# Two-layer graph attention on one core: the first batch's adjacency tiles converted on ScalarE beside the weight setup

## The chip, the cores and the metric

The kernel runs on one core of a Trainium2 chip. The metric is the device time of one execution in microseconds (us), as the median of several runs; lower is better. The engines are named as in the profile: PE (TensorE), DVE (VectorE), ACT (ScalarE), POOL (GpSimd) and SP, whose queue issues the DMAs here.

## The reference, cut to what matters

There are 16 batches of 1024 nodes with 64 features, and a 0/1 adjacency matrix `adj` (16 x 1024 x 1024, int32, about 8 neighbours in a row beside the diagonal). Layer 0 is graph attention with 8 heads, layer 1 graph attention with additive scores; each is followed by a residual and a layer norm.

```python
# layer 0: per head, over neighbours alone
q, k, v = x @ Wq + bq, x @ Wk + bk, x @ Wv + bv
scores = leaky_relu(q @ k.T / sqrt(64) + edge_bias[adj], 0.2)
attn = softmax(where(adj > 0, scores, -1e9))
x = layernorm(x + (attn @ v) @ Wp + bp)
# layer 1
hp = x @ lin_w.T + lin_b
e[i, j] = a . leaky_relu(W1 hp_i + W2 hp_j, 0.2)
x = layernorm(x + elu(softmax(where(adj > 0, e, -9e15)) @ hp))
```

The query and key weights only meet as products (`Wq Wk^T`, `Wq bk`, `Wk bq`, `bq . bk`), and so do `Wv` and `Wp`. The kernel forms these products once, ahead of the batches.

## The kernel before

**Setup.** The weights come in by DMA and are transposed on PE (`wqT`, `wkT`, `wvT`). Then a loop over the 8 heads (lines 107 to 124) forms the products in PSUM and DVE copies them out: `aqk` (64 x 64 per half, L118), `wvp` (L119), `qb` (L122), `wc1` (L124), and `wc8` (L121). `wc8[p, i, h, j]` is the column `Wq bk` of head `h`, where `i == j`, and zero elsewhere, for `i`, `j` below 8; it is cleared by a memset on POOL, and then each head writes 8 columns in each of two halves of the partitions, one instruction a column. The products go through a PSUM pool `ps_c` of 4 banks, two banks a head, so PE comes back to a bank when DVE has read it. Behind the loop come the scores' constants (`wc_row`, `wcb`), layer 1's weights (`lin2`, `w1h`, `w2d`, `rows_b` at L182), and the tables of the sparse form (`wz`, `rep_q`, `ident_b`, `no_diag`). The scratch of the setup is in the pool `tmp`. It and `ps_c` are closed at the end of the setup, and the pools of the groups (`per`, `dbl`, `sml`, the PSUM pools) are opened after that.

**Turning a batch's adjacency into lists** (`prepare`, L307 on). `adj` comes in 16 tiles of 128 rows x 512 columns, in two halves `hs` of 8 tiles. A tile `ad` (L300) has 4 buffers; load `k + 4` is issued after conversion `k`. Each is converted from int32 to bf16 (L325):

```python
nc.vector.tensor_scalar(ab[:, T, :, :], ad, 1.0 - TINY, 0.0, ALU.subtract, ALU.max)
```

which makes a one into `TINY` = 2^-20 and a zero into zero. In half of the tiles POOL clears the diagonal (L328). `ab` holds the 8 tiles of a half and has one buffer. PE sums the tiles of a half, weighted by `wz`, into `pat` (L334, 8 matmuls of 512 columns), DVE makes sort keys `ka` of it (L339), and then the lists of neighbours by max and match-replace instructions (L345 to L383). The lists go to DRAM (`col_d`, `slot_d`) and come back spread over the partitions (`cb` L468, `rows_s` L416). In the middle of its sorting, a batch issues the next batch's loads of `xs`, `dg` (the diagonal) and the first four `ad` tiles.

**The groups.** Eight groups of 128 rows per batch and layer. DVE turns `cb` into 0/1 columns `f` (L480), PE gathers the neighbours' features by matmuls with them (`pg`, L504), then come the scores, exponentials, weights and sums. The order of all engines in this part is written out by hand (a manual schedule): `prepare(0)` and `finish(0)` in full first, then the loop over the groups, with layer 1 of a batch 12 groups behind its layer 0, and `prepare` of the next batch cut into pieces between them. The setup ahead of that is ordered by the scheduler. Each engine does its instructions in the order in which they stand.

If a batch doesn't fit the sparse form, flags (`bad`) make the kernel run a second, dense path at the end; with these inputs it isn't run.

Of the kernel before, what the change touches and what calls it, by code (L numbers as in the profile page):

```python
# [9 lines left out]
F32 = mybir.dt.float32  # L10
I32 = mybir.dt.int32
AF = mybir.ActivationFunctionType
ALU = mybir.AluOpType
# [9 lines left out]
GR = 8  # L23
# [5 lines left out]
TINY = 2.0**-20  # L29
# [4 lines left out]
def kernel(  # L34
# [4 lines left out]
    nc = tc.nc  # L39
    B, N, D = x.shape  # L40
    H = edge_bias.shape[1]
    HD = H * D
    P = 128
# [7 lines left out]
    dram = ctx.enter_context(tc.tile_pool(name="dram", bufs=2, space=bass.MemoryType.DRAM))  # L51
    fast = ExitStack()
    fst = fast.enter_context(tc.tile_pool(name="fst", bufs=1))
    setup = ExitStack()
    ps_c = setup.enter_context(tc.tile_pool(name="ps_c", bufs=4, space=bass.MemoryType.PSUM))
    tmp = setup.enter_context(tc.tile_pool(name="tmp", bufs=1))
    ident = cst.tile([P, P], F32, name="ident")
    make_identity(nc, ident)
    eps = cst.tile([P, 1], F32, name="eps")
# [1 line left out]
    ones = cst.tile([P, P], F32, name="ones")  # L61
    nc.gpsimd.memset(ones, 1.0)


    def sub(n):
        return slice(n * D, n * D + D)
# [6 lines left out]
    def bank(name):  # L73
        return ps_c.tile([P, 4, P], F32, tag="c", name=f"ps_{name}")

    def halves(name, cols_):

        t = fst.tile([P] + cols_, F32, tag=name, name=name)
        nc.gpsimd.memset(t, 0.0)
        return t  # L80
# [21 lines left out]
    QS1 = 1.0 / float(D) ** 0.5  # L102
    aqk = halves("aqk", [2, H, D])
    wvp = fst.tile([P, H, D], F32, name="wvp")
    qb = fst.tile([P, H], F32, name="qb")
    wc8 = halves("wc8", [GR, H, GR])
    wc1 = tmp.tile([1, H], F32, name="wc1")
    for h in range(H):
        c, r = h // 2, sub(h % 2)
        pw = bank(f"h_{h}")  # L110
        pc = bank(f"hc_{h}")
        for n in range(2):
            o = sub(n)
            nc.tensor.matmul(pw[o, 0, 0:D], wqT[r, c, :], wkT[r, c, :], start=True, stop=True)
            nc.tensor.matmul(pw[o, 1, 0:D], wvT[r, c, :], wp_l[r, c, :], start=True, stop=True)
            nc.tensor.matmul(pw[o, 2, 0:1], wkT[r, c, :], bq_c[r, c : c + 1], start=True, stop=True)
            nc.tensor.matmul(pw[o, 3, 0:1], wqT[r, c, :], bk_c[r, c : c + 1], start=True, stop=True)
            nc.vector.tensor_scalar(aqk[o, n, h, :], pw[o, 0, 0:D], QS1, None, ALU.mult)  # L118
            nc.vector.tensor_copy(wvp[o, h, :], pw[o, 1, 0:D])  # L119
            for i in range(GR):  # L120
                nc.vector.tensor_scalar(wc8[o, i, h, i : i + 1], pw[o, 3, 0:1], QS1, None, ALU.mult)  # L121
        nc.vector.tensor_scalar(qb[:, h : h + 1], pw[:, 2, 0:1], QS1, None, ALU.mult)  # L122
        nc.tensor.matmul(pc[0:1, 0, 0:1], bq_c[r, c : c + 1], bk_c[r, c : c + 1], start=True, stop=True)
        nc.vector.tensor_scalar(wc1[:, h : h + 1], pc[0:1, 0, 0:1], QS1, None, ALU.mult)  # L124
    eb1 = tmp.tile([1, H], F32, name="eb1")
    nc.sync.dma_start(eb1, edge_bias[1:2, :])
    nc.vector.tensor_tensor(wc1, wc1, eb1, ALU.add)
# [4 lines left out]
    pw = bank("wcb")  # L132
# [7 lines left out]
    pw = bank("bpv")  # L140
# [15 lines left out]
    pw = bank("ww")  # L156
# [7 lines left out]
    pw = bank("lin")  # L164
    for n in range(2):
        o = sub(n)
# [7 lines left out]
    pw = bank("ub")  # L174
# [5 lines left out]
    pw = bank("rows_b")  # L180
# [53 lines left out]
    jrow = fst.tile([P, SEG // P], F32, name="jrow")  # L234
    nc.gpsimd.iota(jrow, [[-P, SEG // P]], base=SEG, channel_multiplier=-1, allow_small_or_imprecise_dtypes=True)

    bad = cst.tile([P, 1], F32, name="bad")
    nc.vector.memset(bad, 0.0)
    root = fst.tile([P, 1], F32, name="root")
# [16 lines left out]
    MULT = 4  # L256
    XX = mybir.AxisListType.X

    per = fast.enter_context(tc.tile_pool(name="g_per", bufs=1))
    dbl = fast.enter_context(tc.tile_pool(name="g_dbl", bufs=2))  # L260
    sml = fast.enter_context(tc.tile_pool(name="g_sml", bufs=4))
    ps_g = fast.enter_context(tc.tile_pool(name="ps_g", bufs=2, space=bass.MemoryType.PSUM))
    ps_s = fast.enter_context(tc.tile_pool(name="ps_s0", bufs=2, space=bass.MemoryType.PSUM))
    ps_p = fast.enter_context(tc.tile_pool(name="ps_p", bufs=2, space=bass.MemoryType.PSUM))
    ps_z = fast.enter_context(tc.tile_pool(name="ps_z", bufs=1, space=bass.MemoryType.PSUM))

    def by_rows(ap, n):
        return ap[n * 512 : n * 512 + 512, :].rearrange("(t r) d -> r t d", r=D)
# [40 lines left out]
    def prepare(b):  # L309
# [10 lines left out]
        for hs in range(2):  # L320
            ab = per.tile([P, NT, 2, SEG], BF16, tag="ab", name=f"ab_{b}_{hs}")
            for T in range(NT):
                ad = ads.pop(hs * NT + T)

                nc.vector.tensor_scalar(ab[:, T, :, :], ad, 1.0 - TINY, 0.0, ALU.subtract, ALU.max)  # L325
                if T % 4 // 2 == hs:
                    own = ab[:, T, T // 4, ts(T % 2, P)]
                    nc.gpsimd.tensor_tensor(own, own, no_diag, ALU.mult)  # L328
                load(hs * NT + T + 4)
                if T % 2:  # L330
                    yield "sums" if T == NT - 1 else None
            pat = ps_z.tile([P, 2, SEG], F32, tag="z", name=f"pat_{b}_{hs}")
            for T in range(NT):
                nc.tensor.matmul(  # L334
                    pat.rearrange("p a c -> p (a c)"), wz[:, P - NGT - NGT * T : 2 * P - NGT - NGT * T],
                    ab[:, T, :, :].rearrange("p n (t r) -> p t n r", r=D), start=(T == 0), stop=(T == NT - 1),
                )
            yield "keys"
            nc.vector.scalar_tensor_tensor(  # L339
                ka[:, 2 * hs : 2 * hs + 2, 0:SEG], pat, float(KEY), revc.unsqueeze(1).to_broadcast([P, 2, SEG]),  # L340
                ALU.mult, ALU.add,
            )
            yield
            for s in range(2 * hs, 2 * hs + 2):
                nc.vector.max(lst[:, s, 0:8], ka[:, s, 0:SEG])  # L345
                nc.vector.match_replace(kb[:, s, 0:SEG], lst[:, s, 0:8], ka[:, s, 0:SEG], -1.0)
                yield
# [114 lines left out]
    class Tiles:  # L462


        def load(self, t):
            nm = f"{self.b}_{self.layer}_{t}"
            self.cb[t] = cb = dbl.tile([P, NSEG, 2, NQ, WIN], BF16, tag="cb", bufs=3, name=f"cb_{nm}")
            nc.sync.dma_start(  # L468
                cb.rearrange("p s n q k -> p (s n q k)"),
                edges[self.b][t].rearrange("s n q k -> (s n q k)").unsqueeze(0).to_broadcast([P, NSEG * 2 * NQ * WIN]),  # L470
            )
# [382 lines left out]
    class Lists:  # L854


        def __init__(self):
            def parts():
                for b in range(1, B):
                    yield from prepare(b)  # L860
                    yield

            self.work = parts()
            self.done, self.part, self.side = 0, None, []
# [16 lines left out]
    with tc.manual_schedule(engines={getattr(mybir.EngineType, e) for e in order}):  # L881
        for _ in prepare(0):
            pass
# [10 lines left out]
        for g in range(NT * B + LAG + 7):  # L894
            u = g - LAG
            b, t = divmod(g, NT)
# [472 lines left out]
```

## Time and profile before

| | |
|---|---|
| time, median of 3 runs | 2506.59 us (2506.02 to 2509.31) |
| the profiled execution's own time | 2508.34 us |
| its span | 2506.5 us |
| busy, share of the span | PE 92%, PE weight load 78%, DVE 77%, ACT 58%, POOL 40% |
| the conversions L325 | 256 on DVE, 35.6 to 2106.2 us, median 422 ns |
| loads of `ad` (L300) | 256 of 256 KB, on SP's queue |
| first gather matmuls (L504) | at 94 us |

The span is the time from the profile's first instruction to its last; the profiled execution's time has in addition what lies around it. Rows of the timeline give start and duration in us, engine, line, operation, what is written and read, and in brackets how long the engine was idle before, and what ended that. A chain of waits follows from the last instruction back to what released each step. Rows of the page's groups have busy us in total and mean ns of one after the bar.

### The profile page before, as it was taken

To read this page: it belongs to the slowest core of one execution; us is meant where nothing else is said; L and a number is where in the kernel's file an instruction comes from. 1 tells how busy PE (TensorE), PEld (TensorE's weight loads), DVE (VectorE), ACT (ScalarE), POOL (GpSimd) and SP (SyncE) were. 2 spreads that over 40 slices of the span, in tenths; PEclk is the share of its full clock that TensorE was granted. 3 is DMA by queue.
4 is the path that set the end of the run, shared out by engine and by line. 5 is a ranking of instruction groups with operands and counts; after the bars stand their busy time and mean duration, and the time that the engine had idled before them with its cause. 6 is when DMAs were issued, how large, how long until landed. Compare 5 with 4: busy or idle time off the path is not lost.

```text
span 2506.5 us, 111153 instructions
## 1 busy us (share of the span) xinstructions
PE 2296.7 (92%) x48706; PEld 1951.9 (78%) x48706; DVE 1930.4 (77%) x5237; ACT 1450.3 (58%) x4401; POOL 1010.8 (40%) x1490
## 2 busy tenths in 40 slices
PE   5377999999999999999999999999999999999996
PEld 3266778888887888878888887878888887888864
DVE  6586868888887888888788878878787887866543
ACT  0054565666565665656566665656566665666743
POOL 1033433535344353534445353444534444443431
PEclk9988999999999999999999999999999999999998
DMA  3313242333224233323324232332423233231211
GB/s 102 109 43 117 81 143 77 104 116 109 91 81 138 77 117 103 121 77 100 120 77 140 81 119 77 113 107 78 142 86 113 83 111 103 66 96 61 69 38 29
DMA packets 192705, 239.03 MB, mean 95 GB/s; under 512 B 91732, under 2 KB 157332, under 8 KB 192212
## 3 DMA queue, kind: packets, MB, share of 16 engines
q1 hardware_dynamic: 192212, 231.85, 30.3%
q8 instruction: 384, 6.29, 1.0%
q14 instruction: 109, 0.89, 0.1%
HBM read 226.58 MB, written 5.21 MB: 92 GB/s over the span
## 4 chain that ended last, share of the span: by engine, by line
PE 66%; DVE 25%; DMA 3%; ACT 2%; issue 2%; POOL 1%; SPq 0%; POOLq 0%; ACTq 0%; DVEq 0%
PE pg L504 21%; PE s L616 5%; PE pt L523 5%; PE z L668 5%; DVE r L762 4%; PE pz L750 4%; PE pp L658 4%; PE pa L801 4%; PE pq L599 4%; PE pz L756 4%; PE po L684 3%; PE e L776 3%; DVE f L480 3%; DMA ad<-in_adj_dram 2%; PE pat L334 2%
## 5 line engine op out<-in xcount | busy, mean ns | idle before, releaser
L504 PE MATMUL pg<-f,x 128*64 128x272 bf16 (+2 forms) x13312 | 806.1, 273 | 40.4 <-DVE f L480 34.6
L504 PEld LDWEIGHTS <-x 128*64 128x64 bf16 x13312 | 662.8, 109 | 119.2 <-issue 73.8
L650 POOL TENSOR_TENSOR ls<-ls,den 128x480 f32<-128x480 f32 x256 | 298.5, 1166 | 579.8 <-DVE den L649 577.0
L510 ACT COPY xg<-pg 128x448 f32<-128x448 f32 x512 | 271.8, 531 | 392.4 <-PE pg L504 392.2
L480 DVE TENSOR_SCALAR f<-cb,jrow 128x2176 bf16<-128x2176 bf16 x512 | 409.0, 843 | 1.2 <-DMA cb<-col_d 1.0
L642 ACT ACTIVATE ls<-ls,mx 128x120 f32<-128x120 f32 x1024 | 391.2, 386 | 0.0
L524 ACT COPY xn<-pt 120x512 f32<-120x512 f32 x512 | 277.9, 598 | 22.7 <-PE pt L523 21.0
L523 PE MATMUL pt<-ident,xg 128*120 128x128 f32 x2048 | 269.6, 274 | 0.4
L761 ACT ACTIVATE r<-pz 128x480 f32<-128x480 f32 x256 | 132.2, 568 | 220.3 <-PE pz L756 220.3
L523 PEld LDWEIGHTS pt<-ident,xg 128*120 128x120 f32 x2048 | 229.4, 138 | 7.3 <-ACT xg L510 2.8
L489 POOL COPY xg<-xT 128x64 f32<-128x64 f32 x256 | 98.8, 396 | 307.1 <-PE pt L523 307.1
L762 DVE SCALAR_TENSOR_TENSOR r<-pz,r 128x480 f32<-128x480 f32 x256 | 155.9, 651 | 74.9 <-ACT r L761 74.6
L624 DVE TENSOR_TENSOR sc<-s,rowc 128x480 f32<-128x480 f32 x256 | 155.5, 649 | 71.2 <-PE s L616 69.3
L642 ACT ACTIVATION_READ_ACCUMULATOR ls<-ls,mx 128x1 f32 x1024 | 194.5, 190 | 0.0
L558 POOL TENSOR_TENSOR rs<-mv,eps 128x2 f32<-128x2 f32 x128 | 32.3, 253 | 379.0 <-DVE den L649 299.4
L632 DVE SCALAR_TENSOR_TENSOR ls<-sc 128x480 f32<-128x480 f32 x256 | 175.7, 686 | 0.0
L633 DVE TENSOR_REDUCE mx<-ls 128x4 f32<-128x480 f32 x256 | 167.2, 653 | 8.8
L756 PEld LDWEIGHTS pz<-rw,ub 64*64 64x64 f32 x4096 | 118.8, 133 | 63.2 <-issue 62.2
L600 DVE TENSOR_TENSOR qp<-pq,qb 128x512 f32<-128x512 f32 x128 | 88.2, 689 | 102.2 <-PE pq L599 101.0
L668 PE MATMUL z<-w,xn 120*64 120x64 f32 x4096 | 160.2, 229 | 4.8 <-ACT w L660 4.0
L658 PE MATMUL pp<-ident,ls 128*120 128x128 f32 x1024 | 143.0, 281 | 22.9 <-POOL ls L650 16.0
L668 PEld LDWEIGHTS z<-w,xn 120*64 120x64 f32 x4096 | 139.0, 141 | 28.6 <-ACT w L660 26.0
(212 smaller groups left out, 4092.7 us busy)
## 6 DMA issues: line engine op xcount, KB each, us to landing
cb<-col_d SPq DMA_DIRECT2D x271, 544.0 KB
ad<-in_adj_dram SPq DMA_DIRECT2D x256, 256.0 KB
xs<-in_x_dram SPq DMA_DIRECT2D x32, 128.0 KB
rows_s<-slot_d SPq DMA_DIRECT2D x256, 14.0 KB
out_dram<-o SPq DMA_DIRECT2D x32, 128.0 KB
col_d<-col SPq DMA_DIRECT2D x128, 4.2 KB
dg<-in_adj_dram SPq DMA_DIRECT2D x32, 2.0 KB
slot_d<-slot SPq DMA_DIRECT2D x16, 28.0 KB
```

Source lines behind the costliest of these rows:

```text
L480: nc.vector.tensor_scalar(fj.rearrange("p s n q k -> p (s n q k)"), cb.rearrange("p s n q k -> p (s n q k)"), jrow[:, j : j + 1], None, AL ...
L504: nc.tensor.matmul(pg[sub(n), :, FIRST * a_ + lo : FIRST * a_ + to], self.t3[:, k, 4 * hs + 2 * a_ + j, :], f[j][:, 2 * hs + a_, n, :, lo:to],
L510: nc.scalar.copy(dst, pg)
L523: nc.tensor.transpose(pt[:, q, :], xg[:, 4 * m + q, :], ident)
L524: nc.scalar.copy(self.xn[t][:, ts(m, 4), :], pt)
L632: nc.vector.scalar_tensor_tensor(ls, scs[n], SLOPE, scs[n], ALU.mult, ALU.max)
L642: nc.scalar.activation(ls[:, q, :], ls[:, q, :], AF.Exp, bias=neg[:, q : q + 1], accum_out=den[:, q : q + 1])
L650: nc.gpsimd.tensor_tensor(ls, ls, den.unsqueeze(2).to_broadcast([P, 4, SLOTS]), ALU.mult)
L658: nc.tensor.transpose(pt[:, p, :], ls[:, p, :], ident)
L668: nc.tensor.matmul(zz[sub(n), q, :], xn[:, q, sub(n)], w_[n][:, q // 2, sub(q % 2)], start=True, stop=True)
L756: nc.tensor.matmul(pz[n][sub(c_), p, :], ub[sub(n), 2 * p + c_, :], rw[sub(n), :], start=False, stop=(p == 3))
L762: nc.vector.scalar_tensor_tensor(r, pz[n], SLOPE / (1.0 - SLOPE), r, ALU.mult, ALU.add)
```

## The change

The 16 conversions of batch 0 go from DVE to ACT, as a Relu with the bias `TINY - 1` (a new constant `below`); those of the other batches stay on DVE. The eight one-column writes per half of `wc8` are replaced by one copy of the column per head into `wcv`, and after the loop one product of `wcv` with a table `same` (1 where the two indices of 8 are equal, made by an iota and a compare). The pools of the groups `per`, `dbl`, `sml` and `ps_z` are opened before the setup's scratch `ps_c` and `tmp`, so that the scratch lies behind them and shares no memory with them. The line numbers of the changed kernel are 4 to 12 higher.

```diff
-    setup = ExitStack()
-    ps_c = setup.enter_context(tc.tile_pool(name="ps_c", bufs=4, space=bass.MemoryType.PSUM))
-    tmp = setup.enter_context(tc.tile_pool(name="tmp", bufs=1))
...
+    per = fast.enter_context(tc.tile_pool(name="g_per", bufs=1))
+    dbl = fast.enter_context(tc.tile_pool(name="g_dbl", bufs=2))
+    sml = fast.enter_context(tc.tile_pool(name="g_sml", bufs=4))
+    ps_z = fast.enter_context(tc.tile_pool(name="ps_z", bufs=1, space=bass.MemoryType.PSUM))
+    setup = ExitStack()
+    ps_c = setup.enter_context(tc.tile_pool(name="ps_c", bufs=4, space=bass.MemoryType.PSUM))
+    tmp = setup.enter_context(tc.tile_pool(name="tmp", bufs=1))
...
-    wc8 = halves("wc8", [GR, H, GR])
+    wc8 = fst.tile([P, GR, H, GR], F32, name="wc8")
+    wcv = tmp.tile([P, H], F32, name="wcv")
...
-            for i in range(GR):
-                nc.vector.tensor_scalar(wc8[o, i, h, i : i + 1], pw[o, 3, 0:1], QS1, None, ALU.mult)
...
+        nc.vector.tensor_scalar(wcv[:, h : h + 1], pw[:, 3, 0:1], QS1, None, ALU.mult)
...
+    same = tmp.tile([P, GR, GR], F32, name="same")
+    nc.gpsimd.iota(same, [[1, GR], [-1, GR]], base=0, channel_multiplier=0, allow_small_or_imprecise_dtypes=True)
+    nc.vector.tensor_scalar(same, same, 0.0, None, ALU.is_equal)
+    nc.vector.tensor_tensor(
+        wc8, wcv.unsqueeze(1).unsqueeze(3).to_broadcast([P, GR, H, GR]),
+        same.unsqueeze(2).to_broadcast([P, GR, H, GR]), ALU.mult,
+    )
...
+    below = fst.tile([P, 1], F32, name="below")
+    nc.gpsimd.memset(below, TINY - 1.0)
...
-    per = fast.enter_context(tc.tile_pool(name="g_per", bufs=1))
-    dbl = fast.enter_context(tc.tile_pool(name="g_dbl", bufs=2))
-    sml = fast.enter_context(tc.tile_pool(name="g_sml", bufs=4))
...
-    ps_z = fast.enter_context(tc.tile_pool(name="ps_z", bufs=1, space=bass.MemoryType.PSUM))
...
-                nc.vector.tensor_scalar(ab[:, T, :, :], ad, 1.0 - TINY, 0.0, ALU.subtract, ALU.max)
+                if b:
+                    nc.vector.tensor_scalar(ab[:, T, :, :], ad, 1.0 - TINY, 0.0, ALU.subtract, ALU.max)
+                else:
+                    nc.scalar.activation(ab[:, T, :, :], ad, AF.Relu, bias=below)
```

## The prediction

> **What bounds the kernel now.** I read the page's shares first, then the chain of waits from 0 to 100 us, the timeline of the same stretch for each engine, SP's waits, and the stretch table in steps of 2 us. The page:
>
> ```profile
> PE 2296.7 (92%) x48706; PEld 1951.9 (78%) x48706; DVE 1930.4 (77%) x5237; ACT 1450.3 (58%) x4401; POOL 1010.8 (40%) x1490
> PE   5377999999999999999999999999999999999996
> ACT  0054565666565665656566665656566665666743
> L761 ACT ACTIVATE r<-pz 128x480 f32<-128x480 f32 x256 | 132.2, 568 | 220.3 <-PE pz L756 220.3
> ```
>
> From the fourth slice on TensorE is the bound, and none of that work is touched. Ahead of it lies a prologue of 94 us in which ScalarE has nothing to do. The chain through it (start, us, what):
>
> ```profile
> 17.15 0.23 DVE aqk L118
> 17.37 0.14 DVE wvp L119
> 17.52 0.60 DVE wc L121 x8
> 18.13 0.16 DVE qb L122
> 18.29 0.51 DVE wc L121 x8
> 18.87 0.45 PE ps_h L114 x2
> ...
> 35.55 1.11 DVE ab L325 x3
> ...
> 37.96 4.08 DMA ad<-in_adj_dram
> ...
> 42.55 0.60 PE pat L334
> ...
> 45.77 1.35 DVE ab L325 x4
> ...
> 47.42 4.94 DMA ad<-in_adj_dram
> ...
> 54.95 0.70 DVE ka L339
> ...
> 94.03 5.19 PE pg L504 x52
> ```
>
> One head of the weight loop takes 18.87 - 16.12 = 2.75 us, 1.1 us of it the 16 one-column writes of `wc8`. VectorE's setup ends at 35.55; then come the first half's tiles, then the second half's, each ending in a wait for the last load, and at 54.95 the first key multiply of the second half. From there to the gathers at 94.03 everything hangs on that multiply.
>
> ```profile
> SPq L300 <- DVE ab L325: 45.1, 13, 20.1
> 18.00:20.00 2.00, 1.33 (x16) 1.26 (x17) 1.21 (x15) 0.00 (x0) 0.00 (x0) 1.00 0.25 78
> 20.00:22.00 2.00, 0.93 (x11) 0.76 (x10) 1.86 (x22) 0.00 (x0) 0.00 (x0) 1.00 0.00 0
> 36.98 2.00 PE L334 MATMUL pat<-ab,wz 128*128 128x512 bf16 x4 [1.75 <-POOL ab L328]
> ```
>
> The first row is the load queue waiting for a conversion to free one of the four `ad` buffers, once for 20.1 us. In the stretch rows the last two columns are DMA share and GB/s: the first four tiles are in at about 19 us, then the DMA engines stand still until 36. The last row prices the pattern sums: four in 2.00 us, 0.47 us apart.
>
> **What the Trainium skill says.** "ScalarE: Activation LUTs", section What ACT_TABLE_LOAD costs: an ACTIVATE whose bias is a per-partition pointer takes about 280 ns + 0.833 ns per element, neighbours overlap by 93 ns, a table load takes 1283 ns. The trace's table load is 1.28 us (at 35.65), and 568 ns for 480 elements from PSUM agrees with the estimate 280 + 400 - 93 = 587. For 512 elements I estimate 613 ns in a row, 706 alone. The section Table sets of that page says that relu is in every set, so one load should do; the trace of before has no Relu ahead of the exponentials and can't show it for this first one. "TensorE: Matmul & The Clock Gate", Part 1, gives half rate until about 3.4 us of sustained work. The trace agrees in kind: 0.47 us per pattern matmul at 37 us, and eight in 1.89 us (0.24 each) at 204 us.
>
> **The change, part by part.**
>
> 1. *`wc8` in one product.* Gone: 16 writes per head, 0.60 + 0.51 us in the chain, 128 in all. Added: one 128-row copy per head (`wcv`, like `qb`, 0.08 us as it follows another). Per head -1.1 + 0.08 - 0.06, as the `wc1` write stands ahead of PE's restart in before only: about -1.1. The last head's vector work starts at 28.17 in before; seven heads less 1.1 put it at 20.45. The rest of it, with `wcv`, `wc1` and one `a_two`, takes about 0.8. Then the product itself (128x512, two broadcast operands): no such row; the nearest are `rep_q` 0.67 us and `qp` 0.69; I take 0.67, bounds 0.5 and 1.3. `wc1` + edge bias and two `a_two` stand ahead of `wc_row` too, about 0.4, so `wc_row` comes at about 22.3 against 29.32. The tail from `wc_row` to the end of `rows_b` is 35.55 - 29.32 = 6.23, PE-led, and stays: 28.5. The changed order puts `wz` behind it, 0.2: **the first pattern matmul can start at 28.8.** `same` is an iota on POOL in place of the memset of `wc8` (0.52 us) and a compare on VectorE in front of the heads, about 0.1; the memset of `below` is on an idle POOL: nothing.
>
> 2. *Conversions on ScalarE.* 16 leave VectorE; the other 240 stay. In the built order each waits only for its load, its buffer and the constants; the table load waits for the first tile. First tile landed at about 16.3 (middle of the burst of 14 to 19 us), table load to 17.6, four conversions of 0.61 to about 21.3, the last held by its load. The fifth load starts at 18.2 and lands about 3.2 us after the conversion that freed its buffer (46.1 to 49.30 in before), the others some 1.1 us apart: the eighth conversion ends at about 25.5. That lies 3 us under the weights' tail: the first half costs nothing, and what covers it is part 1's tail up to 28.8; if that ended before 25.5, the loads would be the bound.
>
> 3. *First sum.* All eight matmuls are ready, at half rate 0.58 + 7 x 0.45 = 3.7 us: 28.8 to 32.5. `ab` has one buffer, so conversion 9 waits for the last of them, and behind it on ScalarE wait seven conversions and the copy of `xT`; no other work needs that engine yet. In before conversion 9 also stood behind five key instructions on VectorE (43.24 to 45.69); that is gone.
>
> 4. *Second half.* Conversions 9 to 12 start at 32.6 with tiles long there. The first frees its buffer at 33.3. In before, from the first one's end (46.1) to the start of the last (53.35) was 7.25 us, four loads issued 0.6 us apart and slowed by the next batch's `xs` and `dg` loads behind them. The queue order is the same, so 7.25 stays: last conversion at 40.5. From its start to the key multiply 1.6 us in before (conversion 0.43, POOL's diagonal 0.42, matmul 0.60, gaps); here +0.27 for the slower conversion: **42.4 against 54.95, 12.5 us earlier.**
>
> 5. *After that.* The 39 us of list-making from there to 94.03 and every engine's order in the loops are the same, nothing in them starts by the wall clock, and the next batch's four tiles landed long before use in both. So the 12.5 us should reach the end. Moving the pools moves addresses: the built order shows no added wait in the loops, one removed at a later `ex`. I cost it at nothing; bounds -1 and +2 us.
>
> Sum against the profiled execution: 2508.34 - 12.5 = 2495.8. That execution lay 1.75 us above the median of the runs, 2506.59; against the median **2494.1 us**.
>
> **The rivals.**
>
> *A. The weights' tail doesn't shorten.* If PE or waits of a read-after-write kind set the head's period, not the writes, the setup ends near 35.7, the first sum at 39.4, the key multiply at 49.3: gain 5.7, 2500.9 us. Against it: PE restarts at 18.87, right after VectorE's queue, in every head. If half the saving arrives: gain 9.
>
> *B. More.* The tighter heads keep PE busy enough for full rate: eight sums in 1.9 instead of 3.7 us, gain 14.3; with a head's period of 1.5 us a further 1: gain about 15.5, 2491 us. For it: PE's 1.1 us per head rise from 40% of the period to two thirds. Against: the 5 us of almost unbroken matmuls before 35.2 did not bring it in before.
>
> *C. Slower: ScalarE reads int32 badly.* No row shows this engine taking integers. With c us per tile and no cover, the key multiply comes at 17.6 + 16c + 2.6; it equals 54.95 at c = 2.17 us, and the kernel is slower by 5 us from c = 2.5. At c = 3, 2520 us. Against it: 568 ns in the nearest row and a price that the page states per element whatever the function. VectorE reads the same tiles in 0.42 us.
>
> *D. The clock's phase.* The page shows PEclk at 8 to 9 tenths in the early slices: from the granted clock by stretch I work out some 47 us at half rate between 94 and 300 us. Work that meets this in another phase can gain or lose some windows of 3.4 us, at most 1.7 us each; the runs of before spread by 3.3 us. To turn the sign by 5 us it would need ten more such windows.
>
> *Not what it says.* Were the Relu's 2^-20 inexact, the keys would break or the flags send the kernel to its second path, far slower. I leave 1% for it.
>
> **How the numbers follow.** Main case 0.66, A 0.13, B 0.13, C and the last together 0.05, D turning the sign 0.03. The main case's own bounds (product 0.5 to 1.3, addresses -1 to +2, phase 2 either way, setup 1.5) give 2489 to 2499.5. With B and half of A the range is 2488.5 to 2501. A measurement of this kernel can tell about 0.2% (5 us) from no change. Faster by more: main, B, half of A and a little: 0.87. Within: the rest of A and mild forms of C and D: 0.07. Slower: 0.06.
>
> **What would show it.** In the changed profile: ScalarE busy from about 16 us with 16 activations of about 0.6 us; heads 1.6 to 1.7 us apart; `rows_b` copied at about 28; the longest wait of the load queue for a conversion under 8 us instead of 20.1; the second key multiply near 42; the first gathers near 81.5; the same steps later at a constant distance. I am wrong if the conversions take over 1 us, if the gathers come forward but the end doesn't, or if the sum ahead of conversion 9 starts after 32.

## The result, and the profile after

The changed kernel takes 2497.5 us (median of 7, 2495.07 to 2500.37) against 2506.59 us (7 runs, 2505.05 to 2509.76): ratio 0.9964, 95% interval 0.9955 to 0.9974, so 6.5 to 11.3 us less. The profiled execution took 2495.49 us with a span of 2493.7 us, 12.85 us less than the one of before. The forecast was 2494.1 for the median and 2495.8 for the profiled execution.

The chain of waits of the changed kernel from 0 to 100 us (start, us, what):

```profile
13.50 0.23 DVE aqk L123
...
14.25 0.45 PE ps_h L119 x2
...
17.30 0.23 DVE aqk L123
...
18.05 0.45 PE ps_h L119 x2
...
21.42 0.66 DVE wc L132
...
28.66 0.29 DVE rows_b L193
28.95 0.15 DVE wz L232
29.15 3.61 PE pat L346 x8
32.83 2.04 ACT ab L337 x4
34.86 3.93 DMA ad<-in_adj_dram
...
41.94 0.70 DVE ka L351
...
81.64 4.82 PE pg L516 x52
```

Two heads of the weight loop now take 18.05 - 14.25 = 3.80 us where one took 2.75. The product is one step of 0.66 us. The weights' tail still comes first, but behind `wz` the first sum runs straight through eight converted tiles, and on the way to the second key multiply there is one stretch of loads left, not two. The second key multiply comes at 41.94 instead of 54.95, the first gathers at 81.64 instead of 94.03.

ScalarE's timeline and, from the waits of SP's queue, the row for these loads (us in total, times, longest):

```profile
16.43 1.28 ACT L337 ACT_TABLE_LOAD   x1 [16.43 <-DMA ad<-in_adj_dram]
17.73 1.33 ACT L337 ACTIVATE ab<-ad,below 128x512 bf16<-128x512 int32 x2
...
32.83 2.56 ACT L337 ACTIVATE ab<-ad,below 128x512 bf16<-128x512 int32 x4 [7.78 <-PE pat L346]
...
40.04 0.72 ACT L337 ACTIVATE ab<-ad,below 128x512 bf16<-128x512 int32 x1 [0.50 <-DMA ad<-in_adj_dram]
```

```profile
SPq L309 <- ACT ab L337: 13.7, 9, 7.8
```

A conversion costs 0.64 us in a row of four and 0.72 alone. The engine stands for 7.78 us until the first sum has left `ab`, and the load queue's longest wait, 7.8 us, is that same wait seen from behind.

### The profile page after: what moved, and what is told of

It is laid out like the page before. It is cut to its first block, busy times and chain, and to the rows that moved or that the text cites. A ratio compares the mean times of both kernels' runs of the same rounds, so it can differ in the third digit from the quotient of the medians.

```text
span 2493.7 us, 111023 instructions
## 1 busy us (share of the span) xinstructions
PE 2297.9 (92%) x48706; PEld 1955.1 (78%) x48706; DVE 1914.7 (77%) x5103; ACT 1461.3 (59%) x4417; POOL 1010.7 (41%) x1491
## 4 chain that ended last, share of the span: by engine, by line
PE 68%; DVE 23%; ACT 3%; DMA 3%; issue 2%; POOL 1%; SPq 0%; POOLq 0%; ACTq 0%; DVEq 0%
PE pg L516 21%; PE s L628 5%; PE pt L535 5%; PE z L680 5%; DVE r L774 4%; PE pz L762 4%; PE pp L670 4%; PE pa L813 4%; PE pq L611 4%; PE pz L768 4%; PE po L696 3%; PE e L788 3%; PE pat L346 2%; DVE f L492 2%; DMA ad<-in_adj_dram 2%
```

## The experiments

Two views were tested. *S*: a microsecond won ahead of the first gather is one at the end, and the win has two parts that add up. *G*: part of it is given back in the loops, where TensorE meets its half-rate windows in another phase. Then, what each part needs, and what bounds the prologue now.

**e1: the changed kernel again.** No edit.

> The changed kernel once more, unaltered, to see how far the end varies for one and the same start. Theory S (the start alone counts: a microsecond gained before the first gather matmul is a microsecond at the end): first gather at 81.6 us again, the time 12 us under before on average over the runs, and the stretch from the first gather to the end 2412 us as in both profiles so far (2506.5 - 94.03 = 2412.5; 2493.7 - 81.64 = 2412.1). Rival G (part is given back in the loops, since PE meets its half-rate windows in another phase): on average only 9 us, as the medians of the first comparison have it, and a stretch after the first gather of 2412 to 2417 us, longer where more time is at half rate.

First gather at 81.71 us, second key multiply at 42.22. The ratio to before is 0.9948 (0.993 to 0.9965), 9 to 18 us less; the runs lie between 2491.27 and 2502.04 us. The profiled execution had a span of 2498.2 us, so 2416.5 after the first gather: 4.4 us more than the first profile, with the same start. The expectation's 12 us stands inside this interval, G's 9 us inside it too; the spread over all runs is discussed below.

**e2: the product alone.** Conversions on VectorE (the edit shown, against the changed kernel), and the pools in the old order (as in e4).

```diff
-                    nc.scalar.activation(ab[:, T, :, :], ad, AF.Relu, bias=below)
+                nc.vector.tensor_scalar(ab[:, T, :, :], ad, 1.0 - TINY, 0.0, ALU.subtract, ALU.max)
```

> Only the one-product form of wc8; conversions of batch 0 on VectorE and the pools where they were before. If the weights' loop was held by the column writes: heads 1.9 us apart instead of 2.75, rows_b copied at about 28.9, first conversion at about 29.7 (rep_q now stands ahead of it) instead of 35.55, first gather at about 88.2, 5.9 us under before at the end by theory S, 3 by G. If PE or its waits held the loop (rival A of the prediction): first gather at 94, no gain.

From its chain:

```profile
29.51 1.02 DVE ab L332 x3
...
48.78 0.70 DVE ka L346
...
88.48 5.29 PE pg L511 x52
```

First gather 5.55 us earlier, time 0.9974 (0.9965 to 0.9983) of before, about 6.5 us. The column writes did hold the loop, and rival A, with no gain from the product, falls.

**e3: ScalarE and the pools, `wc8` as before.**

```diff
+            for i in range(GR):
+                nc.vector.tensor_scalar(wc8[o, i, h, i : i + 1], pw[o, 3, 0:1], QS1, None, ALU.mult)
```

> ScalarE's conversions and the moved pools, but wc8 written column by column as before. The weights' tail stays at 35.3 and PE starts the first sum there, with all eight tiles converted long before; from there as in the changed kernel (12.8 us from the first matmul of the first sum to the second key multiply): second key multiply at 48.1, first gather at about 87.8; 6.2 us under before at the end by theory S. So the two parts should add up to the whole, 5.9 + 6.2 = 12.1 (whole: 12.4 at the first gather). If the conversions only help once the weights are short: under 2 us here.

```profile
38.76 1.38 ACT ab L330 x3
...
48.42 0.70 DVE ka L344
...
88.00 5.67 PE pg L509 x52
```

First gather 6.03 us earlier, time 0.9972 (0.9961 to 0.9983), about 7 us. The eight tiles of the first half were converted by 25.7 us and waited for PE. PE began the sum at 33.3 us, in the gaps of the weights' tail and so 2 us before the expected start, but ended it at 38.7, as the expectation has it. So the conversions help without the short weights, and the parts add up: 5.55 + 6.03 = 11.6 of 12.4 us at the first gather.

**e4: the changed kernel with the pools in the old order.**

```diff
-    per = fast.enter_context(tc.tile_pool(name="g_per", bufs=1))
...
     setup = ExitStack()
...
+    per = fast.enter_context(tc.tile_pool(name="g_per", bufs=1))
```

> The changed kernel with the pools opened in the old order, so that the buffers of the groups lie in the setup's scratch. If the move is what lets ScalarE start (built order: its table load now waits for VectorE, PE and all load queues): conversions from about 29 us, first sum ended at about 39.6, second key multiply at 48.9, first gather at about 88.6, 5.5 us under before at the end: the product's part alone is left. If the move is of no account: first gather at 81.6 and 12 us.

ScalarE's timeline:

```profile
29.07 1.28 ACT L337 ACT_TABLE_LOAD   x1 [29.07 <-DVE wz L228]
30.36 2.56 ACT L337 ACTIVATE ab<-ad,below 128x512 bf16<-128x512 int32 x4
```

The engine waits until 29.07 instead of 16.43; the profile names the last of the setup's vector work. First gather at 87.72 (expected 88.6), 0.76 us earlier than with the product alone; time 0.9976 (0.9967 to 0.9985), about 6 us. The move of the pools is thus what makes nearly all of the conversions' share possible.

**e5: product and pools, conversions on VectorE.** The lines shown for e2, with the pools left where the changed kernel has them.

> The one-product wc8 and the moved pools, but the conversions of batch 0 stay on VectorE, where the built order has one of the first half's ahead of layer 1's weights and seven behind rep_q. If it is the engine that matters (VectorE's queue holds the conversions back until the setup is through): conversions 2 to 8 from 29.7 us, second key multiply near 48.3, first gather near 88.0, 6 us under before, so as with the product alone. If the moved pools were enough: first gather near 82, 12 us.

VectorE's timeline:

```profile
29.08 0.69 DVE L234 TENSOR_TENSOR rep_q<-in_q,own_i 128x512 bf16<-128x512 f32 x1
29.68 1.66 DVE L332 TENSOR_SCALAR ab<-ad 128x512 bf16<-128x512 int32 x4
```

Tiles that landed by about 19 us stand behind the setup in VectorE's queue until 29.68; only one of the eight was converted earlier, at 26.20. First gather at 88.05, time 0.9981 (0.997 to 0.9991), about 5 us. With e4: neither the engine nor the pools alone give the second part; both together do. What e5 shows is the place in VectorE's queue that the built order gives them. No run put them further forward, where that engine waits for PE between the heads, so it is not shown that only another engine could do it.

**e7 and e8: twice the conversions.** In e7 each conversion of the first half is made twice, in e8 each of the second.

```diff
+                    if not hs:      # e8: if hs
+                        nc.scalar.activation(ab[:, T, :, :], ad, AF.Relu, bias=below)
```

> The changed kernel with each of the first half's 8 conversions on ScalarE made twice, 4.9 us more on that engine. If the first half lies under the weights' tail, as predicted: the last conversion ends near 27.7 instead of 25, the first sum still starts at 29.2, second key multiply still at 41.9 to 42.2. If the conversions were on the path: 44 to 47.

> The changed kernel with each of the second half's 8 conversions made twice. All of it should show: four conversions of 1.22 us before the last buffer is free, 2.4 us more, and 0.6 for the last one: second key multiply at 45.0, 3 us later than in the changed kernel. If the loads alone set that stretch: 42.5.

ScalarE's timeline in e7, then in e8, then the chain in e8 (one run each; only the traces are read):

```profile
28.11 0.72 ACT L339 ACTIVATE ab<-ad,below 128x512 bf16<-128x512 int32 x1
32.71 2.56 ACT L337 ACTIVATE ab<-ad,below 128x512 bf16<-128x512 int32 x4 [3.88 <-PE pat L348]
```

```profile
32.89 0.72 ACT L337 ACTIVATE ab<-ad,below 128x512 bf16<-128x512 int32 x1 [7.46 <-PE pat L348]
...
43.20 0.72 ACT L339 ACTIVATE ab<-ad,below 128x512 bf16<-128x512 int32 x1
```

```profile
41.83 0.73 ACT ab L339
...
45.10 0.70 DVE ka L353
...
84.70 4.65 PE pg L518 x52
```

In e7 the first half ends at 28.8 us instead of 25.0 (expected 27.7), and nothing moves: second key multiply at 41.93, first gather at 81.57. The cover, forecast at 3 us, held 3.8 us of added work, to within 0.3 us of the start of the first sum. In e8 the key multiply comes at 45.10, 3.2 us later (expected 3), but not by the expected way. The expectation added the longer conversions to the same wait for the loads; in the trace ScalarE converts from 32.89 to 43.92 us without a wait, the loads are always there before it, and the engine itself is the bound. That the two come to the same number is luck. A dear conversion would have cost only in the second half until the cover was gone.

**e6: the second half of the tiles in buffers of its own.**

```diff
-            ab = per.tile([P, NT, 2, SEG], BF16, tag="ab", name=f"ab_{b}_{hs}")
+            if b or not hs:
+                ab = per.tile([P, NT, 2, SEG], BF16, tag="ab", name=f"ab_{b}_{hs}")
...
+                for k in range(2):
+                    fk = dbl.tile([P, NSEG, 2, NQ, WIN], BF16, tag="f", bufs=4, name=f"abf_{k}")
```

> The changed kernel, and the second half of batch 0's tiles converted into two buffers of the f columns, idle at that time, so that conversion 9 need not wait for the first sum to leave ab. By the chain of the prediction conversion 9 then starts as soon as its load is in, near 25.6 us instead of 32.8; the loads come every 1.1 to 1.3 us, the last near 33.5; PE goes from the first sum (29.2 to 32.8, half rate) straight into the second, to 36.4; second key multiply at 36.5 instead of 41.9, first gather at 76.3, 5.4 us under the changed kernel and 18 under before. Rival: the loads are the bound in any case (the next batch's small loads slow the last ones): second key multiply at 39 or later, 3 us or less under the changed kernel.

PE's timeline, and the gathers in the chain:

```profile
29.18 3.60 PE L357 MATMUL pat<-ab,wz 128*128 128x512 bf16 x8 [0.53 <-DVE wz L232]
33.64 3.59 PE L357 MATMUL pat<-abf,wz 128*128 128x512 bf16 x8 [0.86 <-DVE ka L362]
```

```profile
37.27 0.70 DVE ka L362
76.45 4.22 PE pg L527 x52
```

First gather at 76.45, 5.2 us ahead of the changed kernel (expected 5.4), the second key multiply 0.8 us later than expected: both sums share a PSUM bank, so the second waited 0.86 us for the first key multiply, which the expectation had left out. Time 2486.53 us, ratio to before 0.9919 (0.9903 to 0.9935). It is clearly faster than before. It was not timed beside the changed kernel, but its ratio lies below both of that kernel's (0.9964 and 0.9948).

**e9: two steps less on PE's chain.**

```diff
-            pat = ps_z.tile([P, 2, SEG], F32, tag="z", name=f"pat_{b}_{hs}")
+            pat = ps_z.tile([P, 2, SEG], F32, tag="z" if b or not hs else "e", name=f"pat_{b}_{hs}")
...
+        nc.vector.tensor_tensor(
+            wc8, wcv.unsqueeze(1).unsqueeze(3).to_broadcast([P, GR, H, GR]),
```

> The kernel with the second half apart, and two steps of its new chain taken off: the wc8 product stands behind the scores' constants (ahead of layer 1's copies) instead of ahead of wc_row, and the second sum has the PSUM bank of the e tiles, so it need not wait for the first key multiply (0.86 us of idle PE there). If PE's chain is the bound: first sum at 28.8, second sum from 32.4 to 36.0, second key multiply at 36.1, first gather at 75.3, about 1.1 us earlier. If the loads and ScalarE are the bound by now (the last conversion ended at 35.1 in the kernel with the second half apart, and POOL, PE and the wait for them take 1.2 us more): 36.4 at best, and little of the two steps shows. The time: 19 us under before, 1 under the kernel with the second half apart, which the timing cannot tell.

PE's timeline, then the chain:

```profile
28.92 3.60 PE L353 MATMUL pat<-ab,wz 128*128 128x512 bf16 x8 [0.53 <-DVE wz L228]
32.31 2.01 PE L353 MATMUL pat<-abf,wz 128*128 128x512 bf16 x7
35.62 0.38 PE L353 MATMUL pat<-abf,wz 128*128 128x512 bf16 x1 [1.30 <-POOL abf L347]
```

```profile
14.19 5.89 DMA ad<-in_adj_dram
20.10 0.73 ACT ab L344
20.85 3.33 DMA ad<-in_adj_dram
...
29.11 3.53 DMA ad<-in_adj_dram
...
36.04 0.70 DVE ka L358
```

The chain has changed hands. It no longer passes through the weights at all, but through four rounds of a load and the conversion that frees its buffer, from 14.19 us on; PE waits 1.30 us for the last tile. The expectation had 36.1 us for the key multiply if PE's chain is the bound, and 36.4 at best if the loads and ScalarE are. It came at 36.04, the number of the first on the path of the second: seven matmuls of the second sum took 2.01 us, where e6 has eight in 3.59, so PE was through early. So it is the chain that decides here, not the number. First gather at 75.66, 0.8 us ahead of e6. Time 2489.42 us, ratio 0.9934 (0.9921 to 0.9948): the timing does not tell it from e6.

**S or G.** Span less the first gather's start, from eleven profiles, in us: before 2412.5; changed 2412.1 and 2416.5 (e1); e2 2413.0; e3 2410.3; e4 2412.6; e5 2412.3; e6 2410.5; e7 2417.5; e8 2414.1; e9 2413.2. Starts from 75.7 to 94.0 us leave this stretch in the same band of 7 us, with the earliest starts (e6, e9) not above the others. The timings say the same. Over the eight comparisons with five runs or more (the first one, e1 to e6, e9) the medians lie 3.8 to 19.6 us under before, where the starts are 5.5 to 18.4 us earlier; added up, it is 83.0 us against 84.5. Some of them share their runs of before, and single ones are off by up to 3.3 us either way: for the changed kernel 9 and 14 us against 12.4 and 12.3. A share of a quarter that is given back, as G has it, is not seen; one of a few per cent could hide in the scatter. What is seen is a scatter of the loops from execution to execution.

The cause of that scatter is not shown. In the two profiles of the changed kernel the granted clock is 0.85 against 0.83 from 82 to 262 us and 1.00 against 0.96 from 262 to 300 us, which would be an estimated 180 x 0.02 + 38 x 0.04 = 5 us if PE were the bound throughout, about the 4.4 us. But e7, with the longest stretch of all (2417.5), has the same 0.85 and 1.00 there as the first profile, with 2412.1. So the clock of these 218 us does not account for the scatter.

## Why the prediction was right, point by point

**The bound.** That the prologue's chain moves the end one for one held: 12.4 us at the first gather, 12.85 in the profiled executions, against 12.5 forecast. The closeness is in part luck. At the gathers two misses cancel: the key multiply came 0.46 us before its forecast (part 4), and the rest took 0.6 us longer (part 5). And e1's profiled execution, with the same start, was only 8.2 us under that of before. The forecast for the median, a ratio of 0.9950, lies just outside the first interval and inside that of e1 (0.993 to 0.9965). One reading is too wide: the page's PE row has 7 tenths in the third and fourth slices, and 9 only from the fifth, so TensorE is not yet the full bound where the loops begin.

**Part 1, the product.** Direction and sum right, the period per head off. Forecast: each head 1.1 us shorter; measured 0.85 (1.90 against 2.75 us), since a head's small `wc1` matmul and write and the next pair's copies came into the wait that the column writes had filled. In the 3.80 us of two heads PE now stands for 0.68 us alone, so it is PE that mostly holds the loop; of rival A so much was right. Seven heads at 0.25 us would have cost 1.75 us. That this did not show in the sum is luck: the last two heads, with no matmuls of a next head behind them, came out 0.62 us apart, which the forecast had not foreseen, so that the last head's vector work began at 20.75 (forecast 20.45), `wc_row` at 22.43 (22.3), and the first sum at 29.15 (28.8). The product measured 0.66 us for the 0.67 taken.

**Part 2, the first half under the tail.** Right: table load at 16.43 (16.3), no second table load ahead of the copies and exponentials, last conversion ended at 25.0 (25.5), cover of about 4 us shown by e7. The ACTIVATE price of the Trainium skill's page "ScalarE: Activation LUTs", section What ACT_TABLE_LOAD costs, gave 613 ns in a row and 706 alone; int32 tiles measured 640 and 720, so rival C, slow integers, falls.

**Part 3, the first sum.** 3.6 us at half rate as forecast (3.7) in the first profile. Rival B's faster rate did not come there, but it came in e1, the same kernel, at the end of the first sum. PE's timeline, in the first profile and then in e1:

```profile
29.15 3.60 PE L346 MATMUL pat<-ab,wz 128*128 128x512 bf16 x8 [0.53 <-DVE wz L232]
33.60 1.20 PE L346 MATMUL pat<-ab,wz 128*128 128x512 bf16 x2 [0.86 <-ACT ab L337]
```

```profile
29.23 3.34 PE L346 MATMUL pat<-ab,wz 128*128 128x512 bf16 x8 [0.53 <-DVE wz L232]
33.43 0.39 PE L346 MATMUL pat<-ab,wz 128*128 128x512 bf16 x1 [0.86 <-ACT ab L337]
```

The sum took 3.34 us there, not the 1.9 of rival B, and the key multiply was no earlier (42.22 against 41.94), since behind it the loads decide.

**Part 4, the second half.** 41.94 against 42.4 for the key multiply. The term of 7.25 us from the first freed buffer to the last conversion, carried over from before, measured 40.04 - 33.47 = 6.6; that is the half microsecond by which the chain did better.

**Part 5, the rest.** The list-making took 39.7 us where 39.1 was carried over, mostly in the stretch of stores and reloads of the lists. The move of the pools was costed at nothing, as a move of addresses. As to the loops no cost is seen. But the step left out what the move does for part 2: e4 shows that without it the conversions start at 29.07, and the gain is halved. Part 2 took from the built order that the conversions wait for little, and did not ask what makes that so.

**The range** of 2488.5 to 2501 us held the median and all seven runs of the first comparison.

## What to carry to other kernels

A prologue in which one engine is idle while another has both the setup and the first data's conversion in its queue is worth looking at even in a kernel that is bound elsewhere for most of its time: what was saved there arrived at the end here, within the scatter. Moving such work took two things at once, an idle engine and memory that the setup's scratch does not own; one without the other gave less than a microsecond at the first gather (e4 0.8, e5 0.4, against the product alone). After each step ask what is late next: it went from vector writes to PE's tail and a single buffer, and, when these were gone, to the loads.

## What the runs showed of the hardware

- Eight 512-column bf16 matmuls after a pause took 3.60 us. In e9 the next seven followed at once and took 2.01 us; in e6, after 0.86 us without a matmul, the next eight took 3.59 us again. The gap alone does not decide it: the two profiles of the changed kernel have the same 0.86 us without a matmul behind the first sum, and then 1.20 us for two matmuls in one and 0.39 for one in the other (e7 has 0.39 too). What brings the faster rate is not shown.
- The granted clock of the profile is not the rate of the matmuls in the prologue. In before it stands at 1.00 up to the first gathers, while a pattern matmul took 0.47 us at 37 us and 0.24 at 204 us. In the changed kernel it stands at 1.00 from 36 to 80 us in the first profile and at 0.50 in e1, with the first gathers at 81.6 and 81.7 us. By estimate such a stretch lowers the mean of the whole execution by 44 x 0.5 / 2494 = 0.009. Of the 13 executions of the changed kernel, seven have a mean of 0.973 to 0.976 and six of 0.983 to 0.987; their times are 2496.6 and 2496.9 us on average. The lower mean did not go with a longer time.
- One and the same kernel's loops of 2.4 ms scattered over several us from execution to execution (2412.1 and 2416.5 us in two profiles of the changed kernel), a third to a half of what this change is worth.
